# Attention scores on four row tiles with a plain key tile, in a two-layer graph network

## The chip, the cores and the metric

The kernel runs on one core of a Trainium2 chip. The metric is the device time of one execution in microseconds. The kernel before was run three times: 2893.09, 2893.73 and 2896.85 us, median 2893.73. TensorE is called PE here, its weight loads PEld, VectorE DVE, ScalarE ACT, GpSimd POOL and SyncE SP, as in the profile.

## What is computed

The input is 128 graphs of 128 nodes with 256 features each, and an adjacency matrix of whole numbers for each graph. Two layers follow each other. Layer 0 applies graph attention twice, adds the input, normalises, and applies a feed-forward block (256 to 1024 to 256, with relu), again with a sum and a normalisation. Layer 1 is the part that the change touches:

```python
q = (src @ Wq + bq).reshape(B, N, h, dh).transpose(0, 2, 1, 3)      # h = 8 heads of dh = 32
k = (src @ Wk + bk).reshape(B, N, h, dh).transpose(0, 2, 1, 3)
scores = jnp.einsum('bhid,bhjd->bhij', q, k) / np.sqrt(dh)
attn = softmax(scores, axis=-1)
for r in range(4):
    v_r = (src @ Wv[r] + bv[r]).reshape(B, N, h, dh).transpose(0, 2, 1, 3)
    out = out + jnp.einsum('bhij,bhjd->bhid', attn * (adj == r)[:, None], v_r)
x = ln(src + out.transpose(0, 2, 1, 3).reshape(B, N, D) @ Wo + bo)
```

After it comes a second feed-forward block, with gelu. Everything is in float32.

## The kernel before

**Groups and stages.** The graphs are taken in 32 groups of four (G = 4; T = 512 nodes). A group passes through five stages, each a Python generator: `load`, `gat` (layer 0's two graph attentions), `ff0`, `att` (layer 1's attention) and `ff1`. Several groups are in flight at once, one in each stage.

**What sets the order.** `layers` keeps a heap of planned times. Each stage emits some instructions and then yields a planned time (a `TIMES` entry) after which it is to go on; a new group begins every 100 planned units. PE's and SP's instructions keep this order of emission by added dependencies (PE from planned time 280 on). The order on ACT, DVE and POOL is made by the framework's scheduler, from priorities and its own estimates; each engine then executes its own list strictly in that order. The kernel is built with two arms. An arm for adjacency values that are all 0 or 1 (`BINARY`) runs here; the other (`GENERAL`) is for other values and isn't executed.

**Buffers.** The PSUM tiles named `mm` share a pool of 7 slots of one bank each; one more bank is for `av`. A new tile takes a slot whose earlier tile has been read for the last time, and the first product into it waits for that read.

**The attention stage** (`attention`). The features are transposed through DRAM into `hT`. Products with `wq` (L468) and `wk` (L474) give, in two chunks of 128 features (DC = 2), the transposed queries and keys of all four graphs. DVE writes the queries to `qT` (L469). ACT writes the keys to `kbd` (L476), and does so twice for each chunk: with `c.own` as the scale, which is one on the partitions of one head of a pair and zero on the other's, so that each 64 partitions hold a block-diagonal pair of two heads' keys:

```python
for q in range(2):
    nc.scalar.activation(c.kbd[i][:, :, q], p, AF.Identity, scale=c.own[:, q:q + 1],
                         bias=c.bk_own[q][:, i:i + 1])
```

`weights(b)` computes the softmax numerators of one graph. Four products (L490), two for each of two row tiles of 64 partitions, have 256 columns: two heads at once. They fill two PSUM banks with four heads each. For each bank DVE takes the maxima (L496), ACT the exponentials of four heads with their sums (L500), DVE the reciprocals (L501), and POOL multiplies (L502).

`turned` transposes e for the products with the values: in 32-by-32 blocks on DVE (L288), then by four DMAs to DRAM (L291) and one back (L293), all on SP's queue. In the last group PE transposes instead. `by_relation` multiplies eT with the mask into `m` on DVE (L515). `values` gives the values of the two relations (L531, L532), the second less the first. `weighted` sums eT with the first and m with the second into `av` (L544, four column tiles of 32), which ACT copies to oT (L548). The product with `wo` (L577) is added to the tokens (L578).

In the order of emission `weights(0)` and `weights(1)` come apart, with other stages' products between them; `weights(2)` and `weights(3)` follow the av products of graphs 0 and 1. Around them stand, from other groups: the second feed-forward products (L378) and their adds (L388), the first feed-forward products (L333) with ACT copies (L339, L340, L346, L351), DVE adds (L347, L348) and activations (L354, L360), the graph-attention products (L435, L443, L454) with their rows on ACT (L410, L422) and DVE (L417, L418, L419, L423), and normalisations (L256 to L265).

The parts that the change touches, with what calls them:

Of the kernel before, what the change touches and what calls it, by code (L numbers as in the profile page):

```python
# [12 lines left out]
F32 = mybir.dt.float32  # L13
I32 = mybir.dt.int32
U32 = mybir.dt.uint32
AF = mybir.ActivationFunctionType
# [13 lines left out]
TIMES = {  # L30
    "sums": 5, "ff visits": (2.5, 2.5, 3, 3, 3.25, 3.25, 3.25, 3.25), "ff2": 3,
    "ff first half": 10, "ff half": 5, "row": 16, "gat": 19, "wh": 5.5,
    "gat copy": 2, "qk": 4.5, "scores": 5.5, "turn0": 10, "turn1": 5,
    "v0": 5.5, "av": 9, "v": 4, "wo": 4, "turn": 3, "mask": 3,
    "lead ff0": 26, "lead att": 32, "lead ff1": 32, "affine": 7,
    "store": 25,
# [8 lines left out]

BINARY = dict(
    binary=True, times=TIMES,
    period=100, bufs=dict(T=5, tok=5, m=1, mm=7, v=2),
    begin=dict(load=-87, gat=-51, ff0=48, att=132, ff1=300),
    early={  # L50
        (1, "ff0"): 48,
# [34 lines left out]
def constants(tc, a, c, cst, tmp, ps):  # L86

    nc = tc.nc
    D, DC, R, MW = c.D, c.DC, c.R, c.MW
    T = G * P  # L90
    c.ident = cst.tile([P, P], F32, name="ident")
    make_identity(nc, c.ident)
    c.mhalf = cst.tile([P, G], F32, name="mhalf")
    nc.vector.memset(c.mhalf, -0.5)

    def wload(name, t=None):

        k, m = a[name].shape
        if t is None:
            t = cst.tile([P, k // P, m], F32, name=name)  # L100
        nc.sync.dma_start(t, a[name].rearrange("(c p) m -> p c m", p=P))
        return t

    def on_all_rows(first, n):

        v = a["rows"]
        return bass.AP(tensor=v.tensor, offset=v.offset + first * D, ap=[[0, P], [1, n * D]])

    c.xt, c.at = [], []

    def load_group(g):
        c.xt.append(tmp.tile([P, DC, T], F32, name=f"xt{g}"))
        nc.sync.dma_start(c.xt[g], a["xT"][g])

    def load_mask(g):
        c.at.append(tmp.tile([P, G, P], I32, name=f"at{g}"))
        nc.sync.dma_start(c.at[g], a["adjT"][g])

    m = wload("M", tmp.tile([P, DC, MW], F32, name="m_in"))
    w2T = wload("W2T", tmp.tile([P, DC, D], F32, name="w2T"))  # L120
    load_group(0)
    w1T = wload("W1T", tmp.tile([P, DC, D], F32, name="w1T"))
    load_mask(0)
    load_group(1)
    load_mask(1)

    pa = ps.tile([P, DC, 2], F32, name="mm")
    for kc in range(DC):
        for oc in range(DC):
            nc.tensor.matmul(pa[:, kc], w2T[:, oc, ts(kc, P)], m[:, oc, D:D + 2], start=oc == 0, stop=oc == DC - 1)  # L130
    nc.vector.tensor_copy(m[:, :, D:D + 2], pa)
    c.wx = cst.tile([P, DC, MW], F32, name="wx")
    for fc in range(DC):
        p = ps.tile([P, MW], F32, name="mm")
        for kc in range(DC):
            nc.tensor.matmul(p, w1T[:, kc, ts(fc, P)], m[:, kc], start=kc == 0, stop=kc == DC - 1)
        nc.vector.tensor_copy(c.wx[:, fc], p)

    for g in range(LEAD):
        nc.sync.dma_start(c.y[g], a["x"][g])  # L140
    col = cst.tile([P, a["cols"].shape[1]], F32, name="col")
    nc.sync.dma_start(col, a["cols"])
    c.col = {k: col[:, i:i + n] for k, (i, n) in COLS.items()}
    c.wf1 = wload("wf1")

    def others():

        ln_rows = cst.tile([P, len(KS), 2, D], F32, name="ln_rows")
        nc.sync.dma_start(ln_rows, on_all_rows(0, 8))
        plus = tmp.tile([P, 3, D], F32, name="plus")  # L150
        nc.sync.dma_start(plus, on_all_rows(8, 3))
        nc.vector.tensor_add(ln_rows[:, :3, 1], ln_rows[:, :3, 1], plus)
        c.ln = {k: (ln_rows[:, n, 0], ln_rows[:, n, 1]) for n, k in enumerate(KS)}
        c.wf2 = wload("wf2")
        c.wq = wload("wq")
        c.wk = wload("wk")
        c.wv = wload("wv")
        c.bv = cst.tile([P, R * D], F32, name="bv")
        nc.sync.dma_start(c.bv, on_all_rows(11, R))
        c.wo = wload("wo")  # L160
        c.w1 = wload("w1")
        c.w2 = wload("w2")
        c.kbd = [cst.tile([P, G, 2, P], F32, name=f"kbd{n}") for n in range(DC)]
        c.own = cst.tile([P, 2], F32, name="own")
        nc.vector.memset(c.own, 0.0)
        for q in range(P // Q):
            nc.vector.memset(c.own[ts(q, Q), q % 2:q % 2 + 1], 1.0)
        c.bk_own = [cst.tile([P, DC], F32, name=f"bk{q}") for q in range(2)]
        c.sums = {n: [cst.tile([P, w.shape[-1] // 2], F32, name=f"{n}s{i}") for i in (1, 2, 4)]
                  for n, w in (("wf1", c.wf1), ("w1", c.w1))}  # L170

    return others
# [43 lines left out]
def per_row(v, n):  # L216

    return v[:, :, None].to_broadcast([P, v.shape[-1], n])


def stages_of(tc, a, out, c, pools, plan):
# [237 lines left out]
    def attention(y, g, first, direct):  # L459
# [5 lines left out]
        for i in range(DC):  # L465
# [2 lines left out]
                nc.tensor.matmul(p, c.wq[:, f, ts(i, P)], hT[:, :, f], start=f == 0, stop=f == DC - 1)  # L468
            nc.vector.tensor_scalar(qT[:, i], p, c.col["bq"][:, i:i + 1], SCALE, op0=OP.add, op1=OP.mult)  # L469

        for i in range(DC):
            p = ps.tile([P, G, N], F32, name="mm")
            for f in range(DC):
                nc.tensor.matmul(p, c.wk[:, f, ts(i, P)], hT[:, :, f], start=f == 0, stop=f == DC - 1)  # L474
            for q in range(2):
                nc.scalar.activation(c.kbd[i][:, :, q], p, AF.Identity, scale=c.own[:, q:q + 1],  # L476
                                     bias=c.bk_own[q][:, i:i + 1])

        if not binary:
            adj = ps.tile([P, G, N], F32, name="adj", bufs=1)  # L480
            nc.vector.tensor_copy(adj, at)

        def weights(b):


            scores = [ps.tile([P, DC, 2, N], F32, name="mm") for _ in range(2)]
            for i in range(DC):
                for h in range(2):
                    rows = ts(h, P // 2)
                    nc.tensor.matmul(scores[h][:, i], qT[rows, i, ts(b, N)], c.kbd[i][rows, b],  # L490
                                     start=True, stop=True, tile_position=(h * P // 2, 0))
            e = wk.tile([P, H, N], F32, name="e1")
            for h, p in enumerate(scores):
                p = p.rearrange("p c q n -> p (c q) n")
                nm = sm.tile([P, HC], F32, name="nm1")
                nc.vector.tensor_reduce(nm, p, AX.X, OP.max, negate=True)  # L496
                s = sm.tile([P, HC], F32, name="s1")
                eh = e[:, ts(h, HC)]
                for q in range(HC):
                    nc.scalar.activation(eh[:, q], p[:, q], AF.Exp, bias=nm[:, q:q + 1], accum_out=s[:, q:q + 1])  # L500
                nc.vector.reciprocal(s, s)  # L501
                nc.gpsimd.tensor_mul(eh, eh, per_row(s, N))  # L502
            return e

        def turned(e):
            eT = wk.tile([P, H, N], F32, name="eT")
# [29 lines left out]
        def weighted(ms, v):  # L536

            po = ps.tile([P, DC, N], F32, name="av", bufs=1)

            order = range(RV) if binary else range(RV - 1, -1, -1)  # L540
            for i in range(DC):
                for n, r in enumerate(order):
                    for q in reversed(range(HC)):
                        nc.tensor.matmul(po[ts(q, DH), i], v[:, r, i * P + q * DH:i * P + (q + 1) * DH],  # L544
                                         ms[r][:, q // 2 * HC + i * 2 + q % 2],
                                         start=n == 0, stop=n == RV - 1, tile_position=(0, q * DH))
            oT = wk.tile([P, DC, N], F32, name="oT")
            nc.scalar.copy(oT, po)  # L548
            return oT

        RV = 2 if binary else R
        yield TIMES["qk"]
        es = [weights(0)]
        yield TIMES["scores"]
        es.append(weights(1))
        yield TIMES["turn0"]
        eT = [turned(es[0])]
        yield TIMES["turn1"]
# [4 lines left out]
        for b in range(G):  # L563
# [3 lines left out]
            oT = weighted(ms, v)  # L567

            if b + 2 < G:
                es.append(weights(b + 2))  # L570
            yield TIMES["v"]
            if more:
                v = values(b + 1)
# [25 lines left out]
def layers(ctx: ExitStack, tc: tile.TileContext, a: dict, out: bass.AP, c, plan: dict):  # L599
# [21 lines left out]
    def stage_attention(g):  # L621
        if g == 0:
            folded(nc, c, pools.ps, c.wq, c.col["bq"], "02")
            folded(nc, c, pools.ps, c.wk, c.col["bk"], "02")
            for q in range(2):
                nc.vector.tensor_scalar(c.bk_own[q], c.col["bk"], c.own[:, q:q + 1], None, op0=OP.mult)
            folded(nc, c, pools.ps, c.wv, c.bv, "02", rows=True)
            if plan["binary"]:
                D = c.D
                nc.vector.tensor_sub(c.wv[:, :, D:2 * D], c.wv[:, :, D:2 * D], c.wv[:, :, :D])  # L630
                nc.vector.tensor_sub(c.bv[:, D:2 * D], c.bv[:, D:2 * D], c.bv[:, :D])
            folded(nc, c, pools.ps, c.w1, c.col["b1"], "11")
            c.w1_sums = weight_sums(nc, c, c.w1, "w1")
        x2[g] = yield from attention(x1.pop(g), g, g == 0, g == NG - 1)
# [148 lines left out]
```

## Time and profile before

| | |
|---|---|
| Median of three runs | 2893.73 us |
| The profiled execution's own time | 2891.83 us |
| Its span, first to last instruction | 2890.0 us |
| PE busy | 2787.7 us (96%), 15554 matmul instructions |
| PEld busy | 2166.1 us (75%) |
| ACT busy | 1724.3 us (60%) |
| POOL busy | 1597.4 us (55%) |
| DVE busy | 1504.7 us (52%) |
| DMA, share of 16 engines | 49.1% |
| Granted PE clock, mean | 0.982 |

The profile is of one execution. In its rows, L is the line of the kernel, then come the engine and the operation, and the tiles written and read. In a group of instructions the count follows an x, then busy time in us and the mean length of one in ns, and after a bar the idle time of the engine just before them with what ended it. In a timeline, the columns are start and length in us, engine, line, operation; a bracket gives idle time before the instruction and who released it. A busy time counts overlapping instructions once. Consecutive matmuls overlap in their records, so the distance of their starts tells more than their lengths.

### The profile page before, as it was taken

How to read it: one execution, taken by the hardware profiler on the slowest of the kernel's cores; microseconds unless marked ns; L12 is line 12 of the kernel's file. 1: busy time of each engine (PE TensorE's matmuls, PEld its weight loads, DVE VectorE, ACT ScalarE, POOL GpSimd, SP SyncE). 2: the span in 40 equal slices, each digit the busy share in tenths (PEclk: the TensorE clock that was granted, in tenths of full speed). 3: DMA queues.
4: the chain of work that ended last, by engine and by line, in shares of the span. 5: the costliest groups of instructions: out<-in, count | busy, mean ns of one | idle time of the engine just before them, and what ended most of it. 6: DMA issues, size and time to landing. Idle time of an engine off the chain costs nothing.

```text
span 2890.0 us, 45554 instructions
## 1 busy us (share of the span) xinstructions
PE 2787.7 (96%) x15554; PEld 2166.1 (75%) x15554; DVE 1504.7 (52%) x3072; ACT 1724.3 (60%) x5191; POOL 1597.4 (55%) x1866
## 2 busy tenths in 40 slices
PE   4996999999999999999999999999999999999988
PEld 3764777777877777777777787777778777777756
DVE  5444545545545555554554555555565545555442
ACT  3445566566666666666656666666666675666543
POOL 1434556556655556665655665565566565556553
PEclk7998999999999999999999999999999999999999
DMA  7145454555554556555445545454654544564310
GB/s 275 45 104 121 104 118 106 110 132 127 119 114 107 113 117 139 114 119 118 106 108 131 129 113 125 104 111 117 137 128 107 123 106 111 122 135 106 77 37 15
DMA packets 1156945, 328.69 MB, mean 114 GB/s; under 512 B 903008, under 2 KB 1126752, under 8 KB 1156064
## 3 DMA queue, kind: packets, MB, share of 16 engines
q1 hardware_dynamic: 1156704, 325.68, 49.1%
q8 instruction: 126, 2.06, 0.3%
q14 instruction: 115, 0.94, 0.1%
HBM read 195.97 MB, written 129.62 MB: 113 GB/s over the span
## 4 chain that ended last, share of the span: by engine, by line
PE 71%; DMA 7%; DVE 6%; POOL 5%; ACT 4%; issue 2%; SPq 2%; DVEq 0%; POOLq 0%; ACTq 0%
PE mm L378 25%; PE mm L333 19%; PE mm L531 5%; PE mm L474 4%; PE mm L468 4%; PE mm L490 4%; PE av L544 3%; PE mm L435 3%; PE mm L577 3%; POOL tok L271 2%; DMA zd<-e 2%; SPq L291 2%; DMA eT<-zd 2%; PE mm L454 1%; DMA zd<-T 1%
## 5 line engine op out<-in xcount | busy, mean ns | idle before, releaser
L271 POOL TENSOR_TENSOR tok<-tok,ln_rows 128x512 f32<-128x512 f32 (+1 forms) x596 | 669.5, 1133 | 34.4 <-PE mm L282 11.1
L500 ACT ACTIVATE e<-mm,nm 128x128 f32<-128x128 f32 x1024 | 362.1, 397 | 239.2 <-DVE nm L496 229.6
L378 PE MATMUL mm<-w,fT 128*128 128x256 f32 x2048 | 460.6, 381 | 0.0
L378 PE MATMUL mm<-wf,fT 128*128 128x256 f32 x2048 | 456.6, 381 | 1.5 <-ACT fT L354 1.5
L378 PEld LDWEIGHTS mm<-w,fT 128*128 128x128 f32 x2048 | 386.6, 190 | 74.2 <-issue 24.2
L502 POOL TENSOR_TENSOR e<-e,s 128x512 f32<-128x512 f32 x256 | 269.4, 1053 | 300.5 <-DVE s L501 299.8
L378 PEld LDWEIGHTS mm<-wf,fT 128*128 128x128 f32 x2048 | 386.5, 190 | 64.3 <-issue 9.2
L515 DVE TENSOR_TENSOR m<-eT,am 128x1024 f32<-128x1024 f32 x128 | 186.2, 1454 | 385.2 <-DMA eT<-zd 374.8
L496 DVE TENSOR_REDUCE nm<-mm 128x4 f32<-128x512 f32 x256 | 162.9, 676 | 254.6 <-PE mm L490 254.6
L265 ACT ACTIVATE tok<-tok,nmr,rstd 128x256 f32<-128x256 f32 x480 | 249.9, 603 | 20.1 <-POOL nmr L263 20.0
L531 PE MATMUL mm<-wv,T 128*128 128x512 f32 x512 | 249.3, 610 | 0.0
L352 POOL TENSOR_TENSOR fT<-fT 128x512 f32<-128x512 f32 x128 | 163.3, 1277 | 153.8 <-ACT fT L351 153.8
L500 ACT ACTIVATION_READ_ACCUMULATOR e<-mm,nm 128x1 f32 x1024 | 242.9, 237 | 0.0
L354 ACT ACTIVATE fT<-fT,col 128x512 f32<-128x512 f32 x256 | 170.4, 715 | 118.8 <-DVE fT L348 117.1
L309 POOL TENSOR_TENSOR t<-T 128x256 f32<-128x256 f32 x64 | 47.6, 744 | 321.3 <-DMA T<-zd 321.0
L333 PE MATMUL mm<-T,w 128*128 128x256 f32 x768 | 202.3, 386 | 4.0 <-DMA T<-zd 2.9
L424 POOL TENSOR_TENSOR e<-e,s 128x512 f32<-128x512 f32 (+1 forms) x68 | 68.1, 1002 | 244.4 <-DVE s L423 230.6
L333 PE MATMUL mm<-T,wf 128*128 128x256 f32 x768 | 193.1, 381 | 0.0
L256 DVE BATCH_NORM_STATS2 st<-tok 128x6 f32<-128x256 f32 x480 | 176.7, 409 | 2.4
L333 PEld LDWEIGHTS mm<-T,w 128*128 128x128 f32 x768 | 144.4, 192 | 30.6 <-issue 6.5
L422 ACT ACTIVATE e<-e,nm 128x128 f32<-128x128 f32 x256 | 101.6, 430 | 105.2 <-DVE nm L419 98.8
L333 PEld LDWEIGHTS mm<-T,wf 128*128 128x128 f32 x768 | 146.1, 191 | 21.7 <-issue 0.8
(144 smaller groups left out, 5147.1 us busy)
## 6 DMA issues: line engine op xcount, KB each, us to landing
zd<-e SPq DMA_DIRECT2D x496, 128.0 KB, 4.6
eT<-zd SPq DMA_DIRECT2D x124, 512.0 KB, 4.4
zd<-T SPq DMA_DIRECT2D x364, 128.0 KB, 3.5
T<-zd SPq DMA_DIRECT2D x91, 512.0 KB, 4.2
xt<-in_xT_dram SPq DMA_DIRECT2D x32, 512.0 KB, 5.0
e<-zsd SPq DMA_DIRECT2D x60, 256.0 KB, 3.3
tok<-in_x_dram SPq DMA_DIRECT2D x30, 512.0 KB
out_dram<-tok SPq DMA_DIRECT2D x29, 512.0 KB, 5.4
```

What stands on the lines that cost most here:

```text
L256: nc.vector.bn_stats(st, y[:, b])
L265: nc.scalar.activation(y[:, b], y[:, b], AF.Identity, bias=nmr[:, b:b + 1], scale=rstd[:, b:b + 1])
L271: engine.tensor_tensor(y[:, b:b + n], y[:, b:b + n], v[:, None, :].to_broadcast([P, n, D]), op)
L333: nc.tensor.matmul(p[:, i], win[k][:, ts(f0 + i, P)], hs[k], start=first and i == 0, stop=True, skip_group_check=True)
L352: nc.gpsimd.tensor_add(hi[:, :, 1], hi[:, :, 1], hi[:, :, 0])
L354: nc.scalar.activation(lo[:, i], lo[:, i], func, bias=bin_[:, f0 + i:f0 + i + 1])
L378: nc.tensor.matmul(ys[b // 2][:, b % 2], fT[f][:, ts(b, N)], wout[:, f], start=b % 2 == 0 and n == 0, stop=n == FC - 1, skip_group_check=True)
L496: nc.vector.tensor_reduce(nm, p, AX.X, OP.max, negate=True)
L500: nc.scalar.activation(eh[:, q], p[:, q], AF.Exp, bias=nm[:, q:q + 1], accum_out=s[:, q:q + 1])
L502: nc.gpsimd.tensor_mul(eh, eh, per_row(s, N))
L515: nc.vector.tensor_tensor(m, eT, at[:, b][:, None, :].to_broadcast([P, H, N]), OP.mult)
L531: nc.tensor.matmul(p, hT[:, b, f], wv[:, f, r:r + 2], start=f == 0, stop=f == DC - 1)
```

## The change

- The keys go to one plain tile `kT` (two ACT copies for a group in place of four); `kbd`, `own` and `bk_own` are dropped.
- The scores are products of one head each: four row tiles of 32 partitions, 128 columns, eight products for a graph in place of four. Each row tile has a PSUM bank of its own.
- `weights` takes a list of graphs. Graphs 0 and 1 are one call, and fill four banks; graphs 2 and 3 are one call each, and fill half of each of four banks. In the other arm, all are single.
- The maxima are taken per row tile: four reduces per call. The order of heads in e follows the row tiles, and the index in `weighted` with it.
- The mask product `m` has two buffers.
- The planned times: the pair is emitted 7 units after the projections, where the two graphs were at 4.5 and 10; the first `turned` stays at 20.

The lines of the changed file stand six higher than before from L164 on, and by other offsets from L480 on.

```diff
-    "gat copy": 2, "qk": 4.5, "scores": 5.5, "turn0": 10, "turn1": 5,
+    "gat copy": 2, "qk": 7, "turn0": 13, "turn1": 5,
...
-    period=100, bufs=dict(T=5, tok=5, m=1, mm=7, v=2),
+    period=100, bufs=dict(T=5, tok=5, m=2, mm=7, v=2),
...
+        kT = wk.tile([P, DC, T], F32, name="kT", bufs=1)
         for i in range(DC):
-            p = ps.tile([P, G, N], F32, name="mm")
+            p = ps.tile([P, T], F32, name="mm")
             for f in range(DC):
                 nc.tensor.matmul(p, c.wk[:, f, ts(i, P)], hT[:, :, f], start=f == 0, stop=f == DC - 1)
-            for q in range(2):
-                nc.scalar.activation(c.kbd[i][:, :, q], p, AF.Identity, scale=c.own[:, q:q + 1],
-                                     bias=c.bk_own[q][:, i:i + 1])
+            nc.scalar.activation(kT[:, i], p, AF.Identity, bias=c.col["bk"][:, i:i + 1])
...
-        def weights(b):
-            scores = [ps.tile([P, DC, 2, N], F32, name="mm") for _ in range(2)]
-            for i in range(DC):
-                for h in range(2):
-                    rows = ts(h, P // 2)
-                    nc.tensor.matmul(scores[h][:, i], qT[rows, i, ts(b, N)], c.kbd[i][rows, b],
-                                     start=True, stop=True, tile_position=(h * P // 2, 0))
-            e = wk.tile([P, H, N], F32, name="e1")
-            for h, p in enumerate(scores):
-                p = p.rearrange("p c q n -> p (c q) n")
-                nm = sm.tile([P, HC], F32, name="nm1")
-                nc.vector.tensor_reduce(nm, p, AX.X, OP.max, negate=True)
-                s = sm.tile([P, HC], F32, name="s1")
-                eh = e[:, ts(h, HC)]
+        def weights(bs):
+            n = len(bs)
+            scores = [ps.tile([P, n, DC, N], F32, name="mm") for _ in range(HC)]
+            for j, b in enumerate(bs):
+                for i in range(DC):
+                    for q in range(HC):
+                        rows = ts(q, DH)
+                        nc.tensor.matmul(scores[q][:, j, i], qT[rows, i, ts(b, N)], kT[rows, i, ts(b, N)],
+                                         start=True, stop=True, tile_position=(q * DH, 0))
+            nm = sm.tile([P, HC, n, DC], F32, name="nm1")
+            for q in range(HC):
+                nc.vector.tensor_reduce(nm[:, q].rearrange("p j i -> p (j i)"),
+                                        scores[q].rearrange("p j i n -> p (j i) n"), AX.X, OP.max, negate=True)
+            es = []
+            for j in range(n):
+                e = wk.tile([P, H, N], F32, name="e1")
+                s = sm.tile([P, H], F32, name="s1")
                 for q in range(HC):
-                    nc.scalar.activation(eh[:, q], p[:, q], AF.Exp, bias=nm[:, q:q + 1], accum_out=s[:, q:q + 1])
-                nc.vector.reciprocal(s, s)
-                nc.gpsimd.tensor_mul(eh, eh, per_row(s, N))
-            return e
+                    for i in range(DC):
+                        k = q * DC + i
+                        nc.scalar.activation(e[:, k], scores[q][:, j, i], AF.Exp, bias=nm[:, q, j, i:i + 1],
+                                             accum_out=s[:, k:k + 1])
+                    if q % 2:
+                        some = slice((q - 1) * DC, (q + 1) * DC)
+                        nc.vector.reciprocal(s[:, some], s[:, some])
+                        nc.gpsimd.tensor_mul(e[:, some], e[:, some], per_row(s[:, some], N))
+                es.append(e)
+            return es
...
-                                         ms[r][:, q // 2 * HC + i * 2 + q % 2],
+                                         ms[r][:, q * DC + i],
...
-        es = [weights(0)]
-        yield TIMES["scores"]
-        es.append(weights(1))
+        es = weights((0, 1)) if binary else weights((0,)) + weights((1,))
         yield TIMES["turn0"]
...
-                es.append(weights(b + 2))
+                es += weights((b + 2,))
```

More of the change, by code (lines that the diff above doesn't have):

```diff
@@ L162, in others @@
         c.w2 = wload("w2")
[L163 to L168, printed above, removed]
         c.sums = {n: [cst.tile([P, w.shape[-1] // 2], F32, name=f"{n}s{i}") for i in (1, 2, 4)]
@@ L624, in stage_attention @@
             folded(nc, c, pools.ps, c.wk, c.col["bk"], "02")
-            for q in range(2):
-                nc.vector.tensor_scalar(c.bk_own[q], c.col["bk"], c.own[:, q:q + 1], None, op0=OP.mult)
             folded(nc, c, pools.ps, c.wv, c.bv, "02", rows=True)
```

## The prediction

> **What bounds the kernel now.** I read first the page's head and busy shares, then busy time by stretch, the groups of instructions by shape, and last the order of time of one group of four graphs.
>
> ```profile
> span 2890.0 us, 45554 instructions
> PE 2787.7 (96%) x15554; PEld 2166.1 (75%) x15554; DVE 1504.7 (52%) x3072; ACT 1724.3 (60%) x5191; POOL 1597.4 (55%) x1866
> ...
> 1396.70:1482.00 85.30, 85.30 (x482) 66.69 (x482) 45.36 (x94) 54.45 (x165) 50.53 (x59) 1.00 0.52 119
> ```
>
> The third line is a stretch of one group: elapsed time, then busy PE, PEld, DVE, ACT, POOL, clock, DMA. PE is busy all of it. From the fourth group to the 29th the q products come every 85.2 us (373.2 to 2504.1, 25 groups) and PE never waits for data. So work taken off PE is worth its full length, until another engine's chain becomes the longer one. Now the operation itself, by shape, and its place:
>
> ```profile
> L490 PE MATMUL mm<-kbd,T 64*128 64x256 f32 x1024 | 147.7, 407 | 2.2 <-ACT kbd L476 2.2
> L544 PE MATMUL av<-m,v 128*32 128x128 f32 x2048 | 104.6, 274 | 0.6 <-DVE m L515 0.6
> ...
> 1410.31 0.38 PE L378 MATMUL mm<-w,fT 128*128 128x256 f32 x1
> 1410.62 1.14 PE L490 MATMUL mm<-kbd,T 64*128 64x256 f32 x8
> 1411.68 0.43 PE L544 MATMUL av<-eT,v 128*32 128x128 f32 x8
> 1411.92 0.40 PE L544 MATMUL av<-m,v 128*32 128x128 f32 x8
> 1412.14 0.40 PE L544 MATMUL av<-eT,v 128*32 128x128 f32 x8
> 1412.36 0.40 PE L544 MATMUL av<-m,v 128*32 128x128 f32 x8
> 1412.69 1.14 PE L490 MATMUL mm<-kbd,T 64*128 64x256 f32 x8
> 1413.76 0.48 PE L378 MATMUL mm<-w,fT 128*128 128x256 f32 x1
> ```
>
> Columns of the last block: start, length, engine, line, what. A product written once is two instructions (512 written, 1024 here). One graph's scores hold PE from 1410.62 to 1411.68, 1.06 us. A full 256-column product starts every 0.216 us (L378, x12 in 2.75 us, the last one's 0.38 included); eight on two row tiles are four pairs, 0.86, and 0.2 is a first weight load that nothing hides (0.10) and the drain before the next mode (0.10). The L544 products, four column tiles of 128 columns, come at 0.218 us for eight: 0.109 per set of four. ACT and DVE of the same stretch:
>
> ```profile
> 1415.27 0.41 ACT L548 COPY oT<-av 128x256 f32<-128x256 f32 x1
> 1415.52 1.33 ACT L410 ACTIVATE e<-e,wh 128x128 f32<-128x128 f32 x4
> 1416.70 0.41 ACT L500 ACTIVATE e<-mm,nm 128x128 f32<-128x128 f32 x1
> ...
> 1416.88 0.69 DVE L417 SCALAR_TENSOR_TENSOR e<-e 128x512 f32<-128x512 f32 x1 [1.25 <-ACT e L410]
> 1418.37 0.66 DVE L419 TENSOR_REDUCE nm<-e 128x4 f32<-128x512 f32 x1
> 1421.19 0.18 DVE L423 RECIPROCAL s<-s 128x4 f32<-128x4 f32 x1 [1.34 <-ACT e L422]
> 1422.77 0.69 DVE L388 TENSOR_TENSOR tok<-tok,mm 128x512 f32<-128x512 f32 x1 [1.39 <-PE mm L378]
> 1423.37 1.24 DVE L288 STREAM_TRANSPOSE e<-e 128x1024 f32<-128x1024 f32 x1
> ```
>
> ACT does eight exponentials (12.51 to 15.27, 0.345 each), oT, the four graph-attention rows L410, then the other eight, to 19.44. DVE's add L388 at 22.77 waits for PE alone; from it DVE runs without a gap to 31.57, and ACT, started by DVE's L348 at 30.14, without a gap to 44.9.
>
> **What the Trainium skill says.** "TensorE: Matmul & The Clock Gate", Part 3 (Packing small matmuls): tiles of different row groups run at once; four row tiles of 512 columns gave 3.07 times. The trace agrees for two: pairs at 0.216, the pace of one. No run here shows four row tiles. Same page, LDWEIGHTS: a load costs by its columns, not its rows; here 187 ns for 64 rows, 190 for 128 (both 128 columns), 110 for 32 columns. "TensorEngine Tiling (Array Packing)", Gotcha 1: row tiles need different PSUM banks; hence four tiles. "TensorE: Matmul & The Clock Gate", Architectural detail: ACT and DVE are strict FIFO; that decides below.
>
> **The change, part by part.** Times are within one group, T0 = 1410.62, the start of the first scores.
>
> PE. A pair: 16 products, 32 instructions, 8 sets of four. Each set 0.109, from the column tiles at L544. For four row tiles this is unknown: not below 0.108 (128 columns at L378's pace), up to 0.214 if only two of four loads run at once, as two are seen to; I take 0.109 and keep the rest for a rival. 0.10 + 0.87 + 0.10 = 1.07 in place of 2 x 1.06: saves 1.06, one mode switch included. A single: 0.10 + 4 x 0.109 + 0.10 = 0.64: saves 0.42, twice. Per group 1.06 + 0.42 + 0.42 = 1.90 us; on 32 groups 61 us, were PE to stay the bound.
>
> kT. Two ACT copies in place of four kbd writes (774 ns): 1.5 us of ACT per group, ahead of T0, where ACT then waits 5.94 us for nm: worth nothing in steady groups (the kbd release stands 5.7 us before its use). Only the first two groups, where L490 waited 2.2 us for kbd, can gain.
>
> Maxima. The pair's four reduces are as the four before (0.64). A single has four of half the size (about 0.4) for two of 0.64: +0.3 us DVE, in a place where DVE idles; the first exponential comes 0.24 earlier. Nothing.
>
> PSUM. Singles take four slots for two. By the order of slots, the first reuse comes after the pair at the first unit's side product of ff0, 6.2 us after the scores' end, and needs four exponentials (which are scheduled across both graphs): 2.3 us. After the last single 3.6 us against some 1.5. Hidden by the av, L378 and L531 products between; without them, the difference would be PE's.
>
> Second m. DVE waits for av before m 8.0 us in all in 128; the eT transfer ends last 374.8. At most 0.06 us a group; taken as nothing.
>
> Queues. SP's order is unchanged; POOL's nearly. ACT's and DVE's are the scheduler's, and here the cost lies. In the built program, 25 of 32 groups (the third to fifth, seventh, ninth to 24th, 26th to 30th) have this: all 16 exponentials of the pair stand ahead of the last of the L410 rows; and on DVE the reciprocal L423, which needs L422's exponentials, stands ahead of the second L388 add and the transposes L288. Before, L410 came after eight. Step by step, from the rows above:
> - last MM of the pair ends at T0+1.14 as before, so the first exponential starts at 12.51 as before.
> - 16 exponentials, oT, four L410 are the same sum, 6.93: last L410 ends about 19.59 (before 16.85).
> - L417, L418, L419: 2.1 (16.88 to 19.03 less a reciprocal): 21.72.
> - L422: 1.75 (19.44 to 21.19): 23.52; reciprocal 0.09: the L388 add starts at 23.61. Before 22.77; PE would have allowed 21.7. DVE, and the chain behind it, is 0.84 late while PE is 1.06 early.
>
> What is late next: DVE's work has no gap, so L348, then ACT's (no gap either) L351 and L360, POOL's nmr, and m and v are all 0.84 later. PE meets them at three places, with what the semaphore records leave it before: L333's last product (needs the L351 copy) 0.47; av of graph 0 (needs v) 0.66; the third L378 product (needs L360's fT) 0.26, of which 0.04 is the wait's own latency. At the last, PE starts 0.84 - 0.22 = 0.62 later than before, counted from T0. PE waits 1.06 + 0.84 - 0.43 = 1.47 at L333 and then 0.42 + 0.62 - 0.41 = 0.63 at L378: 2.10 given back of 1.90. After that only the last single's saving is kept as such: net per group +0.62 - 0.42 = +0.20.
>
> Other groups: three (sixth, eighth, 25th) have the reciprocal seven instructions later and the fT activations ahead of a normalisation; there PE stays the bound: -1.9 each. The 31st has no graph-attention rows: up to -1.9. First two and last, which wait on transfers and on single chains: kT helps up to 2, the interleaved exponentials finish graph 0 up to 2.8 later. Those four together at -2, between -6 and +3.
>
> Sum: 25 x 0.20 - 3 x 1.9 - 2 = -2.7 us. The profiled execution took 2891.83 (span 2890.0); the median of the runs is 2893.73, 1.90 or 0.07% above. Forecast 2893.73 - 2.7 = 2891.
>
> **Rivals.** *PE keeps the gain.* The bound stays PE if the chain above is shorter by 2 us than I count, say if the reads of different banks let the exponentials run faster. For it: PE is 100% busy, all other engines under 65%. Against: the FIFO order is fixed in the program, and 0.345 an exponential held in 1024. It gives 2893.73 - 1.9 x 30 = 2837; a chain shorter by half that, 2865. *Slower: the four row tiles don't reach 0.109.* If two of four loads run at once, a set costs 0.214; the pair holds T0's chain 8 x 0.105 = 0.84 longer, the last single adds 0.42: +1.46 a group, on 25 groups 36, others -2: 2928. It decides from about 0.13 a set (12 x 0.021 = 0.25 a group, 6 us on top). For it: only two were seen at once. Against: the 3.07 times, and that one 128-row load costs what one 64-row load does. *The stall is there and PE's gain is smaller or larger by 0.25 a group*: belongs to the forecast's own range, 25 x 0.25 = 6 either way, the four odd groups 4: 2881 to 2902.
>
> **How the numbers follow.** Forecast 0.62, its own range 2881 to 2902; PE keeps all or much of the gain 0.16; slower tiles 0.20; 0.02 for a PSUM wait that I count as hidden. About 0.2% (5.8 us) is what a measurement of this kernel can tell. Of the forecast's share 0.18 is faster, 0.34 same, 0.10 slower. Faster 0.34, same 0.34, slower 0.32. The range leaves out the full PE gain (0.11) and the worst tiles (0.07): 2855 to 2920.
>
> **What would show it.** Right: the scores' groups x2048, eight instructions of a single spaced so that it takes 0.64 and a pair 1.07; PE idle of some 1.4 us before L333's last product of ff0 on the L351 copy and 0.6 before the first half of its L378, in 25 groups, near 50 us in all; DVE's L423 wait on ACT now just ahead of the transposes; period 85.4 in most groups and 83.3 in three. Wrong: PE without such waits and a period of 83.3 throughout; or a pair of 1.9.

## The result, and the profile after

The changed kernel takes **2919.42 us** (median of 4 runs, 2913.93 to 2924.12) against 2893.41 for the kernel before (now the median of four runs): a ratio of 1.0086, 95% interval 1.0067 to 1.0106. A second series of the same kernel, taken with the experiments below, gave 2922.16 us and 1.0103 (1.0090 to 1.0116). It is slower by about 1%, where the forecast had 2891, a little faster than before. The profiled execution is that of 2924.12 us; its span is 32.3 us longer than the one before. Line numbers are those of the changed kernel: up to the attention code they are six lower than before (L490 of the scores is now L485, the rows L410 are L404, the adds L388 are L382, the transposes L288 are L282, the copies L351 are L345).

The head of the page and its busy shares:

```profile
span 2922.3 us, 47504 instructions
...
PE 2756.2 (94%) x16578; PEld 2146.2 (73%) x16578; DVE 1519.8 (52%) x3193; ACT 1674.7 (57%) x5127; POOL 1598.6 (55%) x1866
```

PE is busy for 31.5 us less than before and the span is 32.3 us longer: PE now idles some 64 us more. The scores themselves, in order of time for PE (a pair of graphs, then in another place of the same group a single):

```profile
1427.15 1.17 PE L485 MATMUL mm<-kT,T 32*128 32x128 f32 x32
1428.25 0.42 PE L546 MATMUL av<-eT,v 128*32 128x128 f32 x8
...
1476.92 0.73 PE L485 MATMUL mm<-kT,T 32*128 32x128 f32 x16
1477.58 1.98 PE L533 MATMUL mm<-wv,T 128*128 128x512 f32 x4
```

From start to the next product's start the pair holds PE 1.10 us and a single 0.66. The forecast had 1.07 and 0.64, from 0.109 us per set of four. The difference, 0.44 for four sets, is 0.11 a set: the four row tiles do run at once. So the saving was there: 1.02 + 2 x 0.40 = 1.82 us a group, 58 in all. (The busy time falls by less. By my estimate, 13 us more are lost to the half clock, which counts as busy, and at some 80 waits the record of the last instruction runs to its end, 0.38 us, and not to the next start, 0.22: another 13.) What became of the saving is read from PE's order of time in the 19th group, and from the waits of the weight loads (PEld) in the whole run (columns: us in total, times, longest):

```profile
1712.88 1.03 PE L327 MATMUL mm<-t,wf 128*128 128x256 f32 x4
1715.08 1.13 PE L327 MATMUL mm<-t,wf 128*128 128x256 f32 x4 [1.17 <-ACT fT L345]
...
1717.91 1.13 PE L372 MATMUL mm<-wf,fT 128*128 128x256 f32 x4
1719.40 2.86 PE L372 MATMUL mm<-wf,fT 128*128 128x256 f32 x12 [0.37 <-ACT fT L354]
```

```profile
PEld mm L327 <- ACT fT L345: 53.2, 29, 2.1
PEld av L546 <- DVE v L534: 25.1, 31, 5.0
PEld mm L372 <- ACT fT L354: 16.1, 23, 0.8
```

Before, the same three waits came to 1.5, 10.4 and 2.0 us. PE waits exactly at the three places where the forecast had put the waits: at the last product of L327 on the copy L345, at av on v, and at the third product of L372 on the activation L354. In this group they are 1.34 us (from 1713.74, four instructions after 1712.88, to 1715.08) and 0.63 (to 1719.40, four instructions after 1717.91 being 1718.77); the forecast had 1.47 and 0.63.

But the groups differ. The 26 steady ones (fourth to 29th) fall in four kinds by the order that the scheduler gave ACT and DVE. T0 is the start of the first scores, times are in us, and the period is the distance to the next group's q products; "first transpose" is DVE's L282 on the first graph's weights, which follows the second L382 add. "The walk" is the prediction's list of steps on ACT and DVE; the lines are named as in the changed kernel, also for the one before.

| kind | groups | L411 us | second L382 add | first transpose | usual period |
|---|---|---|---|---|---|
| before, all | 26 | 0.69 | T0+12.15 | T0+12.75 | 85.05 (mean 85.23) |
| forecast for the 25 | | 0.69 | T0+12.99 | T0+13.6 | 85.44 |
| 1: as the walk has it | 6 | 0.72 | 13.12 | 13.70 | 85.37 |
| 2: L411 beside POOL's multiply | 9 | 1.28 | 13.68 | 14.27 | 85.92 and more |
| 3: L382 between L412 and L413 | 8 | 0.71 | 13.58 | 14.17 | 85.85 |
| 4: L417 behind the transposes | 3 | 1.26 | 12.66 | 13.26 | 84.0 to 84.7 |

Kind 2, in the 16th group: the last row of L404 on ACT, and what follows on DVE.

```profile
1435.69 0.50 ACT L404 ACTIVATE e<-e,wh 128x128 f32<-128x128 f32 x1
...
1435.66 0.18 DVE L502 RECIPROCAL s<-s 128x4 f32<-128x4 f32 x1 [0.63 <-ACT e L498]
1436.22 1.28 DVE L411 SCALAR_TENSOR_TENSOR e<-e 128x512 f32<-128x512 f32 x1 [0.39 <-ACT e L404]
...
1440.73 0.18 DVE L417 RECIPROCAL s<-s 128x4 f32<-128x4 f32 x1 [1.78 <-ACT e L416]
1440.83 0.67 DVE L382 TENSOR_TENSOR tok<-tok,mm 128x512 f32<-128x512 f32 x1
...
1435.92 1.04 POOL L503 TENSOR_TENSOR e<-e,s 128x512 f32<-128x512 f32 x1 [0.36 <-DVE s L502]
```

The rows end at T0+9.04, as forecast (8.97). Then L411 takes 1.28 us instead of 0.69. POOL's last multiply of the pair, released by the reciprocal just ahead of it, runs from 1435.92 to 1436.96; L411 ends 0.54 after that. All thirteen L411 that took 1.26 to 1.28 (the nine, the three of kind 4, and one in the 30th group) stand so. In kinds 1 and 3 the multiply ends 0.17 after L411's start, and L411 takes 0.71 or 0.72. In kind 3, in the 15th group, the time goes elsewhere: the first L382 add, now ready at that moment, stands between the second and third of the operations that ACT waits for.

```profile
1350.39 0.71 DVE L411 SCALAR_TENSOR_TENSOR e<-e 128x512 f32<-128x512 f32 x1 [1.25 <-ACT e L404]
1351.13 0.69 DVE L412 SCALAR_TENSOR_TENSOR e<-cap,e 128x512 f32<-128x512 f32 x1
1351.74 0.68 DVE L382 TENSOR_TENSOR tok<-tok,mm 128x512 f32<-128x512 f32 x1
1352.34 0.68 DVE L413 TENSOR_REDUCE nm<-e 128x4 f32<-128x512 f32 x1
```

Some groups lose more, up to 88.1. In three of them (14th, 16th and 18th) and in the 30th the granted clock falls to a half after the stall; in the 30th it does so once more, after a later wait of 2.27 us at L276. Busy time by stretch in the 16th group (columns: PE, PEld, DVE, ACT, POOL busy, clock, DMA share, GB/s):

```profile
1452.90:1456.30 3.40, 1.34 (x12) 0.89 (x16) 2.75 (x3) 3.40 (x10) 3.40 (x4) 1.00 0.89 131
1456.30:1459.70 3.40, 3.40 (x50) 2.69 (x43) 0.66 (x2) 3.40 (x10) 3.40 (x4) 0.50 0.51 146
```

**The sum.** Against the 85.23 mean of before, the six groups of kind 1 lost 3.0 us (2.3 of it in one that fell to half clock), the nine of kind 2 lost 14.0, the eight of kind 3 lost 6.6, and the three of kind 4 gained 2.9: 20.7 together. The third group took 94.0 us instead of 85.05 (+8.9), the 30th 89.65 instead of 85.74 (+3.9), the 31st gained 1.3; the first two together, and the tail, are even within 0.2. That is the 32.3. In the third group the q products wait for the end of v, which stands on DVE behind an m that waits for its eT transfer, and they then run at half clock for 6.8 us:

```profile
291.10 1.22 DVE L517 TENSOR_TENSOR m<-eT,am 128x1024 f32<-128x1024 f32 x1 [6.82 <-DMA eT<-zd]
292.24 0.68 DVE L534 TENSOR_TENSOR v<-mm,bv 128x512 f32<-128x512 f32 x1
...
292.98 3.78 PE L462 MATMUL mm<-T,wq 128*128 128x512 f32 x4 [3.00 <-DVE v L534]
```

### The profile page after: what moved, and what is told of

Read it like the earlier page. It is cut to its first block, busy times and chain, and to the rows that moved or that the text cites. A ratio compares the mean times of both kernels' runs of the same rounds, so it can differ in the third digit from the quotient of the medians.

```text
span 2922.3 us, 47504 instructions
## 1 busy us (share of the span) xinstructions
PE 2756.2 (94%) x16578; PEld 2146.2 (73%) x16578; DVE 1519.8 (52%) x3193; ACT 1674.7 (57%) x5127; POOL 1598.6 (55%) x1866
## 4 chain that ended last, share of the span: by engine, by line
PE 55%; ACT 13%; DVE 11%; DMA 10%; issue 4%; SPq 4%; POOL 2%; DVEq 0%; ACTq 0%; POOLq 0%
PE mm L372 22%; PE mm L327 11%; PE mm L533 5%; ACT e L498 4%; DMA eT<-zd 4%; SPq L285 3%; PE av L546 3%; PE mm L462 3%; PE mm L469 3%; ACT tok L259 3%; PE mm L577 2%; DVE st L250 2%; DMA zd<-e 2%; DMA zd<-T 2%; PE mm L429 2%
## 5 line engine op out<-in xcount | busy, mean ns | idle before, releaser
L265 POOL TENSOR_TENSOR tok<-tok,ln_rows 128x512 f32<-128x512 f32 (+1 forms) x596 | 669.4, 1132 | 33.5 <-DVE T L282 11.5
L372 PE MATMUL mm<-wf,fT 128*128 128x256 f32 x2048 | 464.1, 383 | 8.6 <-ACT fT L354 7.4
L372 PE MATMUL mm<-w,fT 128*128 128x256 f32 x2048 | 460.6, 381 | 0.0
L372 PEld LDWEIGHTS mm<-wf,fT 128*128 128x128 f32 x2048 | 386.8, 191 | 73.1 <-ACT fT L354 16.1
L372 PEld LDWEIGHTS mm<-w,fT 128*128 128x128 f32 x2048 | 386.6, 190 | 70.3 <-issue 20.5
L489 DVE TENSOR_REDUCE nm<-mm 128x2 f32<-128x256 f32 (+1 forms) x384 | 171.6, 502 | 250.9 <-PE mm L485 250.9
L418 POOL TENSOR_TENSOR e<-e,s 128x512 f32<-128x512 f32 (+1 forms) x68 | 68.1, 1003 | 342.6 <-DVE s L417 319.5
L498 ACT ACTIVATION_READ_ACCUMULATOR e<-mm,nm 128x1 f32 x1024 | 237.0, 231 | 0.0
L327 PE MATMUL mm<-T,w 128*128 128x256 f32 x768 | 203.9, 388 | 5.8 <-ACT fT L340 2.5
L327 PE MATMUL mm<-T,wf 128*128 128x256 f32 x768 | 193.5, 382 | 2.2 <-ACT e L498 2.1
L327 PEld LDWEIGHTS mm<-T,w 128*128 128x128 f32 x768 | 144.8, 192 | 33.6 <-ACT fT L340 7.1
L327 PEld LDWEIGHTS mm<-T,wf 128*128 128x128 f32 x768 | 146.5, 191 | 23.5 <-ACT e L498 2.5
```

The source lines that it names most:

```text
L265: engine.tensor_tensor(y[:, b:b + n], y[:, b:b + n], v[:, None, :].to_broadcast([P, n, D]), op)
L327: nc.tensor.matmul(p[:, i], win[k][:, ts(f0 + i, P)], hs[k], start=first and i == 0, stop=True, skip_group_check=True)
L372: nc.tensor.matmul(ys[b // 2][:, b % 2], fT[f][:, ts(b, N)], wout[:, f], start=b % 2 == 0 and n == 0, stop=n == FC - 1, skip_group_check=True)
L489: nc.vector.tensor_reduce(nm[:, q].rearrange("p j i -> p (j i)"), scores[q].rearrange("p j i n -> p (j i) n"), AX.X, OP.max, negate=True)
L498: nc.scalar.activation(e[:, k], scores[q][:, j, i], AF.Exp, bias=nm[:, q, j, i:i + 1], accum_out=s[:, k:k + 1])
```

## The experiments

Nine further kernels were run, and the changed one once more. The theory: what costs is the order on ACT and DVE that comes with emitting 16 exponentials at once. The rivals: the row tiles, the pair or the second mask buffer cost by themselves.

**The rows first.** The pair's products and maxima stay; its exponentials are emitted as two eights, and the second eight is tied behind the last graph-attention row.

```
-    "gat copy": 2, "qk": 7, "turn0": 13, "turn1": 5,
+    "gat copy": 2, "qk": 7, "scores": 6, "turn0": 7, "turn1": 5,
...
+            row = nc.scalar.activation(e[:, b], p[:, b], AF.Identity, bias=wh[:, b, k:k + 1])
+        if not direct:
+            c.row = row.ins
...
+                    if j and k == 0 and c.row is not None:
+                        tc.add_manual_dep(x.ins, c.row.name, mybir.DependencyInfo(
+                            mybir.DependencyClass.NoSync, mybir.DependencyReason.DATA), reason="rows first")
...
-        es = weights((0, 1)) if binary else weights((0,)) + weights((1,))
+        pair = weights((0, 1)) if binary else weights((0,))
+        es = [exponentials(*pair[0])]
+        yield TIMES["scores"]
+        es.append(exponentials(*(pair if binary else weights((1,)))[-1]))
```

> The pair's 32 products and four maxima stay as changed; the 16 exponentials are emitted as two eights and the second eight is tied behind the four graph-attention rows, so that the rows stand after five to nine exponentials on ACT in every group. If the order on ACT and DVE is what costs: the chain is back where it was, PE is the bound, its saving of 1.9 us a group shows on some 30 groups: 2893.4 - 57 = 2836 us (2828 to 2850), period about 83.4 us, PE waits on the fT copy near nothing. If the row tiles, the pair or the second mask buffer cost by themselves: 2910 to 2925, as changed.

Measured: **2856.58 us**, ratio 0.9884 (0.9867 to 0.9900). That is 63 us below the changed kernel and 1.2% below the kernel before. One group by stretch, the copy's wait of the whole run, and the second add (the pair started at 1396.33):

```profile
1716.40:1800.00 83.60, 83.53 (x513) 65.65 (x513) 45.76 (x98) 52.34 (x161) 50.34 (x59) 1.00 0.54 120
...
PEld mm L327 <- ACT fT L345: 1.3, 1, 1.3
...
1406.92 0.18 DVE L419 RECIPROCAL s<-s 128x4 f32<-128x4 f32 x1 [1.34 <-ACT e L418]
1407.45 0.69 DVE L382 TENSOR_TENSOR tok<-tok,mm 128x512 f32<-128x512 f32 x1 [0.36 <-PE mm L372]
```

PE is busy all of the group again, its 29 waits for the copy are one, and the add stands at T0+11.12, waiting for PE; the rows come after four to eight of the 16 exponentials. So the row tiles, the pair and the plain keys are not what makes the changed kernel slower. But the time is 20 us above the 2836 expected. The shortest periods are 83.28, which is 1.77 below the usual 85.05; the mean of the 26 is 83.80, so they bring 26 x 1.43 = 37 us and not 49 (26 x 1.9); and the third group still takes 88.9. Of the 12 us between, 4.6 are idle time of PE (8.1 us in these groups against 3.5 before), in some groups before av and near the group's end on the copy L340 and the add L341; the rest was not followed up.

**The order alone, on the kernel before.** Two-row-tile scores as before, but the first two graphs emitted together.

```
-    "qk": 4.5, "scores": 5.5, "turn0": 10
+    "qk": 7, "turn0": 13
-        es = [weights(0)]
-        yield TIMES["scores"]
-        es.append(weights(1))
+        es = [weights(0), weights(1)]
```

> The kernel before with its two-row-tile scores, in which only the first two graphs' scores are emitted together and the turn comes 13 later, so that the 16 exponentials stand ahead of the last graph-attention row as in the changed kernel. If the order costs: the chain is as late as in the changed kernel (0.8 to 1.5 us) and PE saves nothing, so a steady group loses 0.8 and the last single's 0.42 more, 26 x 1.2 = 31, and the third group some 9: 2925 to 2935 us. If the order is harmless: 2888 to 2899.

Measured: **2916.28 us**, ratio 1.0077 (1.0060 to 1.0094): slower with the scores on two row tiles as they were. It is less than expected. L417, the L411 of this kernel, takes 0.70 in every group, and the first transpose stands at T0+13.67 in all 26, 0.92 later than before; the walk of the forecast had 0.84. The usual period is 85.74, 0.69 above before (the forecast's sum without the saved PE time gives 0.84 - 0.22 = 0.62), with the waits in the same three places:

```profile
PEld av L544 <- DVE v L532: 23.8, 31, 3.9
PEld mm L333 <- ACT fT L351: 21.3, 29, 1.3
PEld mm L378 <- ACT fT L360: 10.1, 29, 0.4
```

So this is the forecast's chain in its pure form, without the two additions of kinds 2 and 3 that the changed kernel has, which the expectation had counted in. Seven of the 26 groups take longer, 86.9 to 88.5, with further waits at av (up to 1.25) and at L435 near the group's end (0.77); the mean is 86.26. The third group takes 85.8, as the usual ones do.

**POOL's last multiply out of the way.** The changed kernel, in which the last reciprocal of the pair, and with it POOL's last multiply, comes behind L411 (`c.row` is here that operation, and `c.late` holds the second graph's weights and sums; `turn0` is 7). ACT's order stays.

```
+        def last_multiply():
+
+            e, s, some = c.late
+            x = nc.vector.reciprocal(s[:, some], s[:, some])
+            if c.row is not None:
+                tc.add_manual_dep(x.ins, c.row.name, mybir.DependencyInfo(
+                    mybir.DependencyClass.NoSync, mybir.DependencyReason.DATA), reason="row first")
+                c.row = None
+            nc.gpsimd.tensor_mul(e[:, some], e[:, some], per_row(s[:, some], N))
...
         es = weights((0, 1)) if binary else weights((0,)) + weights((1,))
+        if binary:
+            yield 6
+            last_multiply()
         yield TIMES["turn0"]
```

> The changed kernel once more, as the measure for the next run: 2919 us within 4 by every theory.

> The changed kernel, in which the reciprocal and POOL's multiply of the second graph's last four exponentials are emitted 6 later and tied behind DVE's first operation on the graph-attention scores (L411 of the changed kernel); ACT's order stays. That operation took 1.28 us instead of 0.69 in 12 of the 25 plus 3 groups, always while POOL's multiply of the same buffer pool ran until 0.73 after its start. If the multiply holds it up: the operation takes 0.69 in all groups, the chain is 0.57 shorter in 12 groups, and the time is 7 us below the changed kernel's (3 to 12). If its length has another cause: the operation keeps 1.28 and the time stays within 3 us of the changed kernel's.

Measured in one series: 2922.16 us for the changed kernel, 1.0103 (1.0090 to 1.0116), and **2910.85** for this one, 1.0067 (1.0049 to 1.0085): 11.3 us less, the intervals apart. The group of L411 (last columns: busy us, mean ns of one, idle before), first of the changed kernel, then of this one:

```profile
L411 DVE SCALAR_TENSOR_TENSOR e<-e 128x512 f32<-128x512 f32 x60 | 51.2, 853 | 103.1 <-ACT e L404 103.1
```

```profile
L411 DVE SCALAR_TENSOR_TENSOR e<-e 128x512 f32<-128x512 f32 x60 | 42.4, 707 | 131.4 <-ACT e L404 131.4
```

L411 takes 0.69 in all 26 steady groups. The nine groups of kind 2 have their first transpose at T0+13.66 in place of 14.27. The three of kind 4 have it at T0+11.73 and a period of 83.2, 2.0 below the mean of before, as the forecast had said of them (1.9). The eight of kind 3 stay at 14.13 or 14.14. So the multiply held L411 up. That the add in kind 3 costs its 0.60 is read from the trace; no run took it away.

**Four singles instead of the pair.**

```
-    "qk": 7, "turn0": 13
+    "qk": 4.5, "scores": 5.5, "turn0": 10
-        es = weights((0, 1))
+        es = weights((0,))
+        yield TIMES["scores"]
+        es += weights((1,))
```

> The changed kernel without the pair: all four graphs on four row tiles one at a time, emitted at the times of the kernel before. If the order costs and the row tiles do not: the rows stand behind eight exponentials, PE is the bound and saves 4 x 0.42 = 1.68 us a group, on 30 groups 50: 2843 us (2833 to 2857), period 83.6. If four row tiles hurt outside the scores (longer reads of four banks, PSUM slots held): 2890 or more.

Measured: **2919.12 us**, 1.0104 (1.0082 to 1.0126). The expectation fell. The rows stand behind eight exponentials, and PE does not wait for the copy. It waits in the second single itself:

```profile
1418.86 0.88 PE L485 MATMUL mm<-kT,T 32*128 32x128 f32 x4
1419.95 0.48 PE L485 MATMUL mm<-kT,T 32*128 32x128 f32 x2 [0.21 <-ACT e L498]
1420.65 0.71 PE L485 MATMUL mm<-kT,T 32*128 32x128 f32 x10 [0.21 <-ACT e L498]
1421.28 0.92 PE L372 MATMUL mm<-w,fT 128*128 128x256 f32 x3
```

It holds PE 2.42 us instead of 0.66. A half-filled bank takes a whole slot, and the seven slots don't hold eight half-filled score banks, so the second single's products wait, slot by slot, for the first one's exponentials. 1.76 lost against 4 x 0.40 saved: the shortest period is 85.26, 0.21 above before. That is some 5 of the 24 us of the profiled run; the mean of the 26 groups is 86.04, with four steps at half clock among them (7 us), and the rest was not followed up.

**The singles in shared banks.** To take that wait away, the first two graphs were given the pair's four banks, half each: `weights(b, both, j)` works on `both[q][:, j]`.

```
+        both = [ps.tile([P, 2, DC, N], F32, name="mm") for _ in range(HC)]
-        es = weights((0,))
+        es = [weights(0, both, 0)]
         yield TIMES["scores"]
-        es += weights((1,))
+        es.append(weights(1, both, 1))
```

> The kernel of the four singles, in which the first two graphs share the pair's four full PSUM banks: the first writes the front halves and the second, 5.5 later as before, the back halves. If the four singles gained nothing because the second one waited for the first one's slots (1.77 us a group against 1.68 saved): the wait is gone, PE saves 4 x 0.42 a group, the period is 83.6 us and the time 2843 us (2835 to 2857). If single scores on four row tiles lose for another reason, or a bank that is written and read at once is slow: 2890 or more.

Measured: **2950.70 us**, 1.0200 (1.0171 to 1.0228). The edit did not do what it was for; the wait is there still, and longer:

```profile
PEld mm L482 <- ACT e L492: 56.0, 120, 1.8
```

The program now lets the second graph's products into a bank only when the first graph's exponentials have read it. In the four singles the same wait came to 25.5. It therefore doesn't tell whether singles without that wait would keep their gain; this stays open. It shows only that halves of one bank, emitted apart, don't get around the wait in this program.

**One mask buffer**, in the changed kernel and in the one with the rows first (`m=2` back to `m=1`, nothing else).

> The changed kernel with one mask buffer as before. If the second buffer is worth nothing, as forecast: 2919 us, within 6. If it lets m start earlier and saves something: 2926 or more. If the buffer moved work or transfers into each other's way and that is part of the loss: below 2910.

> The kernel with the rows ahead of the second eight exponentials, with one mask buffer instead of two. If the second buffer is worth nothing where PE is the bound: 2856.6 us within 5. If m waits for the previous av there: 2862 or more.

Measured: 2922.80 us, 1.0110 (1.0093 to 1.0127), and 2858.52, 0.9880 (0.9866 to 0.9895). The second buffer is worth nothing in either, as forecast.

**The pair earlier**, in two steps from the kernel with the rows first: `"qk": 4.5, "scores": 8.5, "turn0": 7`, and the same with `"turn0": 4.5`.

> The kernel with the rows ahead of the second eight exponentials, with the pair and the first eight emitted 2.5 earlier, as the first scores of the kernel before were; the order in the steady groups is the same. If the early pair mends the third group, which has 88.9 us where the kernel before has 85.1: 2853 us (2849 to 2856). If not: 2856.6 within 3.

> The kernel with the rows ahead of the second eight exponentials (2856.6 us), with the pair and the first transpose emitted 2.5 and 5 earlier. If what is left there is the wait for the first eT transfers: the multiplications m and v of the first graph come earlier, the third group's 88.9 us falls to about 85.5, and the time to 2848 (2842 to 2853). If PE's own work is the floor (83.3 a group) in most groups and the order of the other engines gets worse: 2855 or more.

Measured: 2862.84 us, 0.9898 (0.9882 to 0.9915), and **3008.26**, 1.0394 (1.0379 to 1.0409). In the first, the third group falls to 85.9, but it begins at 293.3 instead of 287.3: the loss at the start has only moved into the groups ahead of it. In the second, PE's order is the order of emission, and the earlier transposes pulled the output product L587 ahead of four L327 products in it. PE then waits there for the copy of av, which is behind the exponentials on ACT, and twice per group for the fT copy:

```profile
PEld mm L327 <- ACT fT L345: 108.7, 57, 4.2
...
PEld mm L587 <- ACT oT L557: 58.7, 30, 2.7
```

Both expectations of a gain failed; the first lies 3 us beyond its range for no gain, too. What the start of the run loses with a pair was not settled.

## Why the prediction was wrong

- **The bound, the places and the direction of the walk held.** ("PE never waits for data" did not quite: in five of the 26 groups before, PE waits 0.55 us for v at av, and these take 85.7 to 85.8.) PE saves 1.02 us at the pair (2.12 to 1.10; forecast 1.06) and 0.40 at a single (0.42). The chain on ACT and DVE takes PE's place, and PE waits at L327, av and L372. That the order does it is shown from both sides: with the rows first, and all else in the change kept, the time falls by 63 us; and joining the first two graphs in the emission, which also moves the second one's scores on PE, makes the old kernel slower by 23 without the rest of the change.
- **The step that failed** is "L417, L418, L419: 2.1 ... L422: 1.75; reciprocal 0.09: the L388 add starts at 23.61. DVE, and the chain behind it, is 0.84 late", applied to 25 groups alike. In six groups it was right (T0+13.12 for 12.99; period 85.37 for 85.44), and in the old kernel with that order too (0.92 late). I took the three operations' length from a group where nothing ran beside them or between them. In the new order POOL's last multiply runs beside the first one in nine groups, which adds 0.57, and in eight the first L388 add stands between them, which adds 0.60. DVE kept to its list: in kind 3 ACT waits for L413, which stands behind an add that ACT does not need. The place of that add was to be read in the built program; the first is what the Trainium skill says in "SBUF — State Buffer", SBUF: two separate sides: a DVE operation with two SBUF inputs and a GpSimd operation that reads SBUF take turns on a shared port, each for the whole instruction. The prediction did not ask it of L417, though POOL's multiply follows each reciprocal. The trace agrees: the waiting operation ends 0.54 us after POOL's, in all thirteen.
- **What it cost.** The forecast had the profiled run 2.7 us below before, and it is 32.3 above. Of these 35 us, 19 are in the 23 groups of kinds 1 to 3 (23.6 against 23 x 0.2): about 10 by the two additions (9 x 0.57 + 8 x 0.60), 5 by half clock, and 4 in later waits. The three groups of kind 4 make 2.8, the third 8.7, the 30th 3.7, the rest 0.8.
- **The three groups left to PE**: -1.9 each was forecast and -1.0 measured. The same port: there L411 is held 0.57 by POOL's multiply, and L412 0.96 (1.65 instead of 0.69) by the normalisation L265 behind it on POOL. With the multiply moved they gained 2.0.
- **What a stall does next was left out.** The forecast had priced each stall at its length. Four of them were followed by 3.4 us at half clock, 1.7 us each. In the ninth and 21st groups the late chain also meets L327 and L429 near the group's end: waits of 0.17, 0.70 and 0.28, and periods of 87.7.
- **The first and last groups.** The first two, the 31st and the last were put at -2 together, and came to -1.2. The third and the 30th, which I had counted among the 25, lost 8.9 and 3.9. The third is the largest miss of any one group, and I had no step for it. In the kernel with the rows first it is 3.9; its cause stays open.
- **Zero-cost edits**: the kT copies, the reduces and the second mask buffer cost nothing that shows, as the kernel with the rows first has them all; the mask buffer alone was tried, twice. The PSUM slots are hidden for the pair, as forecast, and they are not for four singles.
- **The rivals.** "The row tiles don't reach 0.109" gave 2928, near the measured time, for a reason that is not there: a set takes 0.11. "PE keeps the gain" described the kernel with the rows first, at 2857 and not 2837: the saving that arrives is 1.4 a group and not 1.9.
- **Luck.** The forecast's own range ended at 2902 and its widest at 2920, so that the measured 2919 lies in the widest (the second series, 2922, just outside); it came there by the additions above and not by the slow row tiles for which that width was left.

## What to carry to other kernels

When work is taken off the bounding engine by emitting two units at once, the other engines' order can change with it. Walk that order through the built program for every variant it has, not for the commonest, and for each operation on that chain ask what runs beside it on POOL and what stands between. Here 36 of PE's 58 us reached the run's time once eight exponentials were tied behind four small row activations.

## What the runs showed of the hardware

- Four 32-row tiles ran at once at the pace of one: 32 instructions took 1.10 us and 16 took 0.66, so 0.11 for each set of four instructions of 128 columns, and 0.22 beside the sets. Each row tile wrote to a bank of its own; no run tried two in one bank. A weight load of 32 rows took 193 ns, where one of 64 took 187 and one of 128 took 190. One instruction of 256 columns starts every 0.216, which is 0.108 for 128.
- A DVE operation with two SBUF inputs (128x512) took 1.28 us instead of 0.69 when POOL's multiply had started 0.3 us earlier; it ended 0.54 after POOL's. With the multiply moved behind it, it took 0.69.
- The granted clock fell in steps of 3.41 us. In the changed kernel 4 of the 29 stalls on the fT copy were followed by one such step at 0.5. The starts of these steps lie whole steps apart (1282.24 to 1456.32, 174.08 us, is 51 of them). The Trainium skill, "TensorE: Matmul & The Clock Gate", Part 1, says that such windows run free of the work, and the trace agrees. Laid over the groups from the fourth to the 30th, the five steps at half clock follow the five steps in which PE was least busy, 1.13 to 1.65 us of 3.41; three with 1.68 were not followed by one. This fits that a stall inside one step brings it on, and one split over two steps does not. It is no sharp limit: in the kernel with the multiply moved, a step with 1.48 was not followed by one. Three steps of the changed kernel (PE busy, clock, DMA share, GB/s), the first two followed by half clock:

```profile
1278.83:1282.24 3.41, 1.21 (x8) 1.00 0.59 84
1626.99:1630.40 3.41, 1.65 (x24) 1.00 0.90 131
2483.73:2487.14 3.41, 1.68 (x8) 1.00 0.97 181
```

- It took no single long gap: in the singles in shared banks, where PE waits three or four times within 3 us for 0.2 to 0.3 each, 12 of the 26 groups had a step at half clock. The busy time alone does not tell it there, as steps with PE busy for 2.45 to 2.77 us were followed by one.
